# Sums in front of the remainders in the last groups of two square layers

## The chip, the cores and the metric

The kernel runs on one core of a Trainium2 chip. The metric is the device time of one execution in microseconds (us). A core has five engines that work side by side, each through its own queue: TensorE (PE, matrix products), VectorE (DVE), ScalarE (ACT), GpSimd (POOL) and SyncE (SP, which issues most of the DMAs here).

## What is computed

A transformer block on 4 batches of 1024 tokens with 256 features: attention with 16 heads, then a feed-forward part, each between a layer norm of its input and a layer norm of its output, with a residual. The change concerns the feed-forward part alone:

```python
def _tlin(x, w, s):
    return jnp.einsum('bsi,oi->bso', x, w) * s
h = jax.nn.silu(_tlin(x, w1_w, w1_s)) * _tlin(x, w2_w, w2_s)
h = jax.nn.gelu(_tlin(h, h1_w, h1_s), approximate=False)
h = jax.nn.gelu(_tlin(h, h2_w, h2_s), approximate=False)
return _tlin(h, w3_w, w3_s)
```

Features go 256 -> 1024 -> 1024 -> 1024 -> 256. `h1` and `h2` are the square layers. All weights `w*_w` are -1, 0 or 1.

## The kernel before

**Stages.** Attention takes the time to about 592 us. Then the feed-forward part runs batch after batch: `gated` (w1, w2, Silu and product), `Layer.run` for `h1`, `Layer.run` for `h2`, `finish` (w3, then the layer norm and the residual). In the first three batches the layer norm's last steps run within the next batch's `gated`; in the last batch (`b == B - 1`) `finish` runs them to the end, block by block, and stores.

**Precision.** [...] So each activation `raw` is split in two: `Operand.high` (line 923) rounds it on ScalarE (`hi`, line 925), `Operand.low` (line 927) takes the remainder `raw - hi` on VectorE (`lo`, line 929). Every product is done with both halves. A tile (`Half`) has 128 partitions x 1024 numbers: two blocks of 128 features by 512 tokens. Tiles come from a ring of free ones: `Half(...)` takes the oldest, `release` puts it back, in the order in which the program is written.

**A square layer** (`Layer`) treats input, weights and output as 2 x 2 blocks, (feature half i, token half j), and uses seven block products (`k` = 0 to 6) in place of eight. Which sums of weight blocks are used is prepared beforehand (`factors`, loaded from HBM into a ring of four slots by `load_factor`); the sums of input blocks are made on VectorE (`t1`, `make2`, `make3`, `make4`, line 941). Every product is done in two groups, `r` = 0 and 1, so a layer has 14 groups, `g` = 0 to 13. A group is 16 matmuls of 128x512 (line 1034) into a PSUM tile `ph`; there are three such tiles.

**Ends of groups.** After groups 6 and 7 a partial sum is kept (`keep_copy`, tile `w`); after groups 8 and 9 block (1,0) goes straight through Gelu (`straight`, tile `c`). After groups 10 to 13 stands `add` (line 1042): VectorE adds PSUM to a kept tile (line 1045), then ScalarE takes the Gelu in two halves (line 1022). Groups 10 and 11 give block (1,1) from `w`, groups 12 and 13 block (0,1) from `u`. Product 6 adds into the PSUM tile that product 5 began, so PE's group 12 (13) may start only when the sum of group 10 (11) has read that tile.

**Splits for the next layer.** While a layer's last groups run, its finished blocks are split for the next one. `ending` (line 1231) builds the lists: `early[g]` is run in group g after its matmuls are issued and before its sum, `extra[g]` after its sum and Gelu. Before the change, `early` holds both operations of a split, `high` then `low`. Half 1 of (0,0) is split in group 10, the halves of (1,0) in 11 and 12; in layer `h2` also half 0 of (1,1) in group 12 and half 1 in group 13, where half 0 of (0,1) follows in `extra`. The last one, half 1 of (0,1), is split in `finish` after the first scaling.

**The output** (`finish`). Four output tiles `pz` of 32 matmuls each (line 1139), token half 0 first. The products of token half 1 read block (1,1) first and (0,1) last. VectorE scales each (line 1144), and in the last batch goes on with the statistics, a root on POOL (line 107), the normalisation, the residual (line 1151) and a store.

Order on an engine is the order in which the program is written; each engine takes its queue from the front.

Of the kernel before, what the change touches and what calls it, by code (L numbers as in the profile page):

```python
# [129 lines left out]
def tile_fast(ctx: ExitStack, tc: tile.TileContext, x, wqk, wv, wo, w1, w1s, w2, w2s, h1, h1s, h2, h2s, w3, w3s, out, bad):  # L130
# [65 lines left out]
    with ExitStack() as actx, ExitStack() as rctx:  # L196
# [764 lines left out]
        def emit(runs):  # L961
            for run in runs:
                run()

        class Layer:
# [36 lines left out]
            def run(self, q, scale, extra, early):  # L1002

                out, at = self.out, {}
                hi, lo = self.high, self.low
                steps = {
                    0: [hi(2, 0), self.t1(1), self.make2(1), lo(2, 0)],
                    1: [hi(2, 1), lo(2, 1), self.make4(0), self.make4(1)],
                    2: [self.make3(0), self.make3(1), hi(3, 0), lo(3, 0)],
                    3: [hi(3, 1), lo(3, 1)],  # L1010
                    4: [hi(4, 0), lo(4, 0)],
                    5: [hi(4, 1), lo(4, 1)],
                    6: [hi(5, 0), lo(5, 0)],
                    7: [hi(5, 1), lo(5, 1)],
                    8: [hi(6, 0), lo(6, 0)],
                    9: [hi(6, 1), lo(6, 1)],
                }

                def gelu(o, i, r, src=None):
                    for j in range(2):  # L1020
                        m = HC // 2 * i + 2 * r + j
                        nc.scalar.activation(o.t[:, j, :], (o.t if src is None else src)[:, j, :], AF.Gelu, scale=scale[:, m : m + 1])  # L1022

                def space(r):
                    at[r] = ps.tile([P, 2, NQ], F32, tag="big", name="ph")
                    return at[r]

                def products(k, r, start):
                    p = at[r]
                    for c in range(HC // 2):  # L1030
                        for j in range(2):
                            w = ring_of[(q + k) % SLOTS][c // 2][:, c % 2, (2 * r + j) * P : (2 * r + j + 1) * P]
                            for n, half in enumerate(self.moving[k].pairs(c)):
                                nc.tensor.matmul(  # L1034
                                    p[:, j, :], w, half,
                                    start=start and c == n == 0, stop=c == HC // 2 - 1 and n == 1, skip_group_check=True,
                                )
                    if r:
                        self.moving[k].release()
                        load_factor(q + k + SLOTS)  # L1040

                def add(n, i, j, r):
                    o = out[n][r]
                    out.setdefault((i, j), []).append(o)
                    nc.vector.tensor_add(o.t, at[r], o.t)  # L1045
                    gelu(o, i, r)

                def keep_copy(n, r):
                    o = Half(n)
                    out.setdefault(n, []).append(o)  # L1050
                    nc.scalar.copy(o.t, at[r])

                def straight(i, r, p):
                    o = Half("c")
                    out.setdefault((i, 0), []).append(o)
                    gelu(o, i, r, p)

                def branch(r):
                    first[r] = at[r]
                    nc.scalar.copy(space(r), first[r])  # L1060

                first = {}

                def second(r):
                    p, at[r] = at[r], first[r]
                    products(1, r, False)
                    at[r] = p
                    straight(0, r, first[r])

                def after(g):  # L1070
                    emit(steps.get(g, ()))
                    emit(extra.get(g, ()))

                space(0), products(0, 0, True), branch(0), after(0)
                space(1), products(0, 1, True), after(1)
                second(0), branch(1), after(2)
                products(2, 0, False), keep_copy("u", 0), after(3)
                second(1), after(4)
                products(2, 1, False), keep_copy("u", 1), after(5)
                for g in range(6, 14):  # L1080
                    k, r = g // 2, g % 2
                    if k == 5:
                        space(r)
                    products(k, r, k == 5)
                    emit(early.get(g, ()))
                    if k == 3:
                        keep_copy("w", r)
                    elif k == 4:
                        straight(1, r, at[r])
                    else:  # L1090
                        add(*(("w", 1, 1) if k == 5 else ("u", 0, 1)), r)
                    after(g)
                return {n: out[n] for n in ((0, 0), (1, 0), (1, 1), (0, 1))}

# [127 lines left out]
        def feed_forward():  # L1222
# [8 lines left out]
            def ending(layer, drop):  # L1231
                for at in ((0, 0), (1, 0), (1, 1), (0, 1)):
                    layer.out[at] = []
                ops = {at: Operand(layer.out[at], drop) for at in ((0, 0), (1, 0), (1, 1), (0, 1))}
                extra = {g: [] for g in range(14)}
                extra[7] += split(ops[0, 0], 0)
                early = {g: split(ops[at], i) for g, at, i in ((10, (0, 0), 1), (11, (1, 0), 0), (12, (1, 0), 1))}
                return ops, extra, early

            def prepared(extra, steps):  # L1240
# [9 lines left out]
            for b in range(B):  # L1250
                last = b == B - 1
                x = {}
                for at in ((0, 0), (1, 0), (0, 1), (1, 1)):
                    x[at] = []
                corner, low = Operand(x[0, 0]), Operand(x[1, 0])
                one = Layer(x, corner, low)
                steps = {g: [] for g in range(NH * HC)}
                if b == 0:
                    for g in steps:
                        steps[g].append(side.take)  # L1260
                    steps[7].append(lambda: until(lambda: "fb" in ffn))
                for g, runs in tails.items():
                    steps[g] += runs
                for g, runs in (
                    (7 if b == 0 else 6, split(corner, 0)), (8 if b == 0 else 7, split(corner, 1)), (9, split(low, 0)), (11, split(low, 1)),
                    (12, [one.t1(0)]), (14, [one.make2(0)]),
                ):
                    steps[g] += runs
                if b == 1:
                    steps[6] += [checks.load, checks.load]  # L1270
                if b == 1:
                    checked(steps, (11,), (13,))
                elif b:
                    checked(steps, (1, 6, 11), (3, 8, 13))
                gated(x, steps)
                until(lambda: made_factors[0] == len(corners) and "fb" in ffn)
                q = 2 * 7 * b
                ops, extra, early = ending(one, False)
                if b == 0:
                    for g in range(3, 12):  # L1280
                        extra[g].append(side.take)
                if b:
                    checked(extra, (3, 4, 10), (5, 6, 12))
                if not last:
                    prepared(extra, prepare(2 * b + 2, to_scalar))
                if b == 0:
                    extra[5].insert(0, lambda: until(lambda: not chain[0]))
                y = one.run(q, scales["h1"], extra, early)
                until(lambda: not chain[0])
                two = Layer(y, ops[0, 0], ops[1, 0])  # L1290
                ops, extra, early = ending(two, True)
                if b:
                    checked(extra, (3, 4), (5, 6))
                if not last:
                    prepared(extra, prepare(2 * b + 3, to_scalar))
                else:
                    for g, step in zip((8, 9), judge()):
                        extra[g].append(step.run)
                early[12] += split(ops[1, 1], 0)
                early[13] = split(ops[1, 1], 1)  # L1300
                extra[13] += split(ops[0, 1], 0)
                emit([two.t1(0), two.make2(0)])
                two.run(q + 7, scales["h2"], extra, early)
                tails = finish(b, ops, {0: split(ops[0, 1], 1)})
# [333 lines left out]
```

## Time and profile before

| what | value |
|---|---|
| median of 3 runs (lowest, highest) | 1232.06 us (1228.26, 1233.94) |
| the profiled execution | 1232.08 us, its span 1230.2 us |
| granted clock of TensorE | 0.987 |
| PE busy in 595.0 to 757.4 us (batch 0) | 159.71 of 162.40 us |
| PE busy in 757.4 to 909.5 us (batch 1) | 151.17 of 152.10 us |
| PE busy in 909.5 to 1061.8 us (batch 2) | 151.34 of 152.30 us |
| PE busy in 1061.8 to 1211.0 us (batch 3) | 148.31 of 149.20 us |
| VectorE and ScalarE busy in batch 2 | 107.59 and 97.63 us |
| one remainder (line 929), one sum (line 1045) | 1.23 us, 1.22 us |
| a rounding (line 925), two Gelu halves (line 1022) | 1.04 us, 1.34 us |

The profile comes from one execution, so the times of its lines belong to the 1232.08 us. A row of the timeline gives the start, the duration, the engine, the line of the program, the operation, output and inputs by name, and in brackets the idle time of the engine before it with what ended that. When instructions of an engine follow closely, a row begins up to 0.1 us before the end of the row before it, so a queue is timed by the steps between starts. The 1.9 us between span and time of the execution lie around the span.

### The profile page before, as it was taken

To read this page: it belongs to the slowest core of one execution; us is meant where nothing else is said; L and a number is where in the kernel's file an instruction comes from. 1 tells how busy PE (TensorE), PEld (TensorE's weight loads), DVE (VectorE), ACT (ScalarE), POOL (GpSimd) and SP (SyncE) were. 2 spreads that over 40 slices of the span, in tenths; PEclk is the share of its full clock that TensorE was granted. 3 is DMA by queue.
4 is the path that set the end of the run, shared out by engine and by line. 5 is a ranking of instruction groups with operands and counts; after the bars stand their busy time and mean duration, and the time that the engine had idled before them with its cause. 6 is when DMAs were issued, how large, how long until landed. Compare 5 with 4: busy or idle time off the path is not lost.

```text
span 1230.2 us, 21266 instructions
## 1 busy us (share of the span) xinstructions
PE 1169.1 (95%) x7994; PEld 710.1 (58%) x7994; DVE 841.5 (68%) x1500; ACT 885.1 (72%) x1049; POOL 209.1 (17%) x279
## 2 busy tenths in 40 slices
PE   7999999999999999999999999999999999999993
PEld 2333333333333333333578888887888878888783
DVE  3485668777687756868685756867578676784755
ACT  3798899878988989999457565576656766566651
POOL 6222035434354432000000000000000000000000
PEclk8999999999999999999999999999999999999997
DMA  4676755756666666453314341344512545125401
GB/s 132 175 183 152 172 148 134 186 135 175 152 162 154 173 168 148 96 140 128 104 34 138 119 156 52 103 171 147 178 59 97 175 156 176 62 82 199 155 7 37
DMA packets 78672, 163.66 MB, mean 133 GB/s; under 512 B 14688, under 2 KB 40928, under 8 KB 78560
## 3 DMA queue, kind: packets, MB, share of 16 engines
q1 hardware_dynamic: 68624, 131.27, 38.7%
q0 software_dynamic: 9408, 30.42, 7.7%
q8 instruction: 65, 1.06, 0.4%
q10 hardware_dynamic: 528, 0.52, 0.2%
q14 instruction: 47, 0.39, 0.1%
HBM read 98.71 MB, written 29.88 MB: 105 GB/s over the span
## 4 chain that ended last, share of the span: by engine, by line
PE 58%; DVE 12%; ACT 12%; SPq 6%; DMA 6%; issue 5%; ACTq 0%; POOL 0%; POOLq 0%; DVEq 0%
PE ph L1034 27%; PE acc L542 9%; PE pg L955 8%; ACT e L535 6%; PE s L534 6%; SPq L482 5%; PE p L321 3%; DVE lo L929 2%; ACT hi L925 2%; PE py L321 2%; DVE top L554 1%; DMA sq<-cq1lo 1%; DMA folded<-top_d 1%; PE pz L1139 1%; DVE w L1045 1%
## 5 line engine op out<-in xcount | busy, mean ns | idle before, releaser
L535 ACT ACTIVATE e<-s 128x1024 f32<-128x1024 f32 x512 | 483.1, 1043 | 53.8 <-PE s L534 44.1
L542 PE MATMUL acc<-e,vaug 128*32 128x512 f32 (+1 forms) x2424 | 258.7, 539 | 2.9 <-POOL vaug L512 2.9
L534 PE MATMUL s<-sq,sk 64*128 64x512 f32 x1024 | 189.3, 446 | 25.3 <-ACT e L535 17.1
L534 PEld LDWEIGHTS s<-sq,sk 64*128 64x128 f32 x1024 | 87.6, 185 | 172.0 <-ACT e L535 142.1
L1034 PE MATMUL ph<-hi,sq 128*128 128x512 f32 x448 | 178.1, 398 | 0.8 <-DVE w L1045 0.8
L1034 PE MATMUL ph<-lo,sq 128*128 128x512 f32 x448 | 176.7, 394 | 0.0
L1034 PE MATMUL ph<-hi,sk 128*128 128x512 f32 x448 | 176.7, 394 | 0.0
L1034 PE MATMUL ph<-lo,sk 128*128 128x512 f32 x448 | 176.4, 394 | 0.0
L107 POOL TENSOR_TENSOR rstd<-ve,minus_half 128x4 f32<-128x4 f32 (+1 forms) x34 | 38.2, 1123 | 740.6 <-DVE ve L105 681.8
L554 DVE TENSOR_TENSOR top<-top,e 128x512 f32<-128x512 f32 x192 | 138.9, 723 | 24.3 <-ACT e L535 18.5
L542 PEld LDWEIGHTS acc<-e,vaug 128*32 128x32 f32 x2424 | 61.8, 109 | 120.5 <-issue 107.8
L929 DVE TENSOR_TENSOR lo<-c,hi 128x1024 fp32r<-128x1024 f32 x48 | 58.4, 1223 | 66.0 <-ACT hi L925 66.0
L929 DVE TENSOR_TENSOR lo<-g,hi 128x1024 fp32r<-128x1024 f32 x48 | 58.8, 1226 | 58.0 <-ACT hi L925 57.7
L1034 PEld LDWEIGHTS ph<-hi,sq 128*128 128x128 f32 x448 | 84.2, 188 | 21.6 <-DVE w L1045 2.1
L1034 PEld LDWEIGHTS ph<-hi,sk 128*128 128x128 f32 x448 | 84.1, 188 | 20.0
L1034 PEld LDWEIGHTS ph<-lo,sk 128*128 128x128 f32 x448 | 84.1, 188 | 19.9
L1034 PEld LDWEIGHTS ph<-lo,sq 128*128 128x128 f32 x448 | 84.2, 188 | 19.1
L1022 ACT ACTIVATE c<-ph,h_scale 128x512 f32<-128x512 f32 x64 | 40.6, 685 | 50.1 <-PE ph L1034 50.1
L321 PE MATMUL p<-xT,wqk_sb 128*32 128x512 f32 x512 | 69.3, 622 | 4.7 <-ACT wqk_sb L209 2.6
L957 ACT ACTIVATE sg<-pg,w_scale 128x512 f32<-128x512 f32 x64 | 43.6, 688 | 35.7 <-PE pg L955 31.9
L1139 PE MATMUL pz<-w_sb,lo 128*128 128x256 f32 x256 | 61.6, 284 | 2.8 <-DVE lo L929 2.8
L958 DVE SCALAR_TENSOR_TENSOR g<-pg,w_scale,sg 128x512 f32<-128x512 f32 x64 | 47.7, 747 | 23.1 <-ACT sg L957 23.0
(183 smaller groups left out, 1735.1 us busy)
## 6 DMA issues: line engine op xcount, KB each, us to landing
sq<-h_f SPq DMA_DIRECT2D x56, 512.0 KB, 3.8
sk<-h_f SPq DMA_DIRECT2D x56, 512.0 KB, 4.5
w<-in_h_dram POOLq DMA_DIRECT2D x32, 256.0 KB, 5.2
h_f<-wr POOLq DMA_DIRECT2D x16, 512.0 KB, 4.3
x<-in_h_dram SPq DMA_DIRECT2D x16, 512.0 KB, 3.6
top_d<-top SPq DMA_DIRECT2D x30, 256.0 KB, 2.5
folded<-top_d SPq DMA_DIRECT2D x30, 256.0 KB, 3.2
h_f<-wr POOLq DMA_DIRECT2D x16, 384.0 KB, 3.7
```

What stands on the lines that cost most here:

```text
L321: nc.tensor.matmul(o[j : j + SLOT, :], w[:, j : j + SLOT], i, **flags)
L482: queue.dma_start(out=stacks[w, i, u][o : o + DH, c0:c1].bitcast(F32), in_=cq[w, m, k][r : r + DH, c0:c1].bitcast(F32))
L534: nc.tensor.matmul(s[:, a, :], stacks[1, g % 2, u][r, c * P : (c + 1) * P], stacks[0, g % 2, u][r, h * NQ : (h + 1) * NQ], start=True, sto ...
L535: nc.scalar.activation(pair(k)[:, u], s, AF.Exp)
L542: nc.tensor.matmul(acc[SLOT * i : SLOT * (i + 1), q0:q1], vaug[g % 2][:, c, i, :], pair(k)[:, i // 2, i % 2, q0:q1], start=c == 0 and q0 = ...
L554: nc.vector.tensor_max(top, top if c > 1 else pair(k - 2)[:, :, :, 0:P], pair(k)[:, :, :, 0:P])
L929: nc.vector.tensor_sub(self.lo[i].t, self.raw[i].t, self.hi[i].t.bitcast(F32))
L955: nc.tensor.matmul(p[:, k, :], homes[n][d][:, m * P : (m + 1) * P], half[:, d, :], start=d == j == 0, stop=d == DC - 1 and j == 1)
L957: nc.scalar.activation(sg, p[:, 0, :], AF.Silu, scale=scales["w1"][:, m : m + 1])
L958: nc.vector.scalar_tensor_tensor(x[i, h][c // 2].t[:, c % 2, :], p[:, 1, :], scales["w2"][:, m : m + 1], sg, ALU.mult, ALU.mult)
L1034: nc.tensor.matmul(p[:, j, :], w, half, start=start and c == n == 0, stop=c == HC // 2 - 1 and n == 1, skip_group_check=True,)
L1139: nc.tensor.matmul(p[:, j, :D], half[:, (t0 + j) * P : (t0 + j + 1) * P], homes["w3"][c], start=c == order[0] and n == 0, stop=c == order[ ...
```

## The change

In groups 6 to 13 the roundings of `early[g]` stay in front of the group's own sum or Gelu, and the remainders move behind it. `early` holds pairs of an operand and a half in place of functions. In layer `h2`, half 0 of block (0,1), which was split after the sum of group 13, joins the list of that group, so that its rounding stands before that group's Gelu. The number of instructions stays the same on every engine. For this shape, ScalarE's order differs in one rounding per batch, VectorE's in the remainders of groups 10 to 13 against the sums; the orders on PE, POOL and SP are the same.

```diff
@@ -1082,13 +1082,16 @@
                     if k == 5:
                         space(r)
                     products(k, r, k == 5)
-                    emit(early.get(g, ()))
+                    for o, i in early.get(g, ()):
+                        o.high(i)
                     if k == 3:
                         keep_copy("w", r)
                     elif k == 4:
                         straight(1, r, at[r])
                     else:
                         add(*(("w", 1, 1) if k == 5 else ("u", 0, 1)), r)
+                    for o, i in early.get(g, ()):
+                        o.low(i)
                     after(g)
                 return {n: out[n] for n in ((0, 0), (1, 0), (1, 1), (0, 1))}
 
@@ -1234,7 +1237,7 @@
                 extra[7] += split(ops[0, 0], 0)
-                early = {g: split(ops[at], i) for g, at, i in ((10, (0, 0), 1), (11, (1, 0), 0), (12, (1, 0), 1))}
+                early = {g: [(ops[at], i)] for g, at, i in ((10, (0, 0), 1), (11, (1, 0), 0), (12, (1, 0), 1))}
                 return ops, extra, early
 
@@ -1296,9 +1299,8 @@
-                early[12] += split(ops[1, 1], 0)
-                early[13] = split(ops[1, 1], 1)
-                extra[13] += split(ops[0, 1], 0)
+                early[12].append((ops[1, 1], 0))
+                early[13] = [(ops[1, 1], 1), (ops[0, 1], 0)]
                 emit([two.t1(0), two.make2(0)])
                 two.run(q + 7, scales["h2"], extra, early)
                 tails = finish(b, ops, {0: split(ops[0, 1], 1)})
```

## The prediction

> **What bounds the kernel now.** I began with the page: per engine, TensorE (PE) is busy for 95% of the span, VectorE (DVE) for 68%, ScalarE (ACT) for 72%. The slices of the feed-forward part (from about 592 us on) show PE at nine tenths or more and its clock at nine, except in the last slice. So two places can pay: the few gaps in PE, and the end, where PE is done and others finish.
>
> ```profile
> PE 1169.1 (95%) x7994; PEld 710.1 (58%) x7994; DVE 841.5 (68%) x1500; ACT 885.1 (72%) x1049; POOL 209.1 (17%) x279
> PE   7999999999999999999999999999999999999993
> L929 DVE TENSOR_TENSOR lo<-c,hi 128x1024 fp32r<-128x1024 f32 x48 | 58.4, 1223 | 66.0 <-ACT hi L925 66.0
> ```
>
> The third line says that a remainder (`lo`) takes 1223 ns and that VectorE sat idle for 66 us in front of 48 of them, waiting for a rounding (`hi`) on ScalarE. Idle time of VectorE costs nothing by itself, so I went on to the timeline of the last layer's groups 10 to 13 (batch 3, `h2`), VectorE and then ScalarE:
>
> ```profile
> 1185.24 1.21 DVE L1045 TENSOR_TENSOR w<-ph,w 128x1024 f32<-128x1024 f32 x1
> 1188.79 1.23 DVE L929 TENSOR_TENSOR lo<-c,hi 128x1024 fp32r<-128x1024 f32 x1 [2.35 <-ACT hi L925]
> 1189.93 1.22 DVE L1045 TENSOR_TENSOR w<-ph,w 128x1024 f32<-128x1024 f32 x1
> 1193.49 1.23 DVE L929 TENSOR_TENSOR lo<-c,hi 128x1024 fp32r<-128x1024 f32 x1 [2.34 <-ACT hi L925]
> 1194.63 1.22 DVE L929 TENSOR_TENSOR lo<-w,hi 128x1024 fp32r<-128x1024 f32 x1
> 1195.77 1.22 DVE L1045 TENSOR_TENSOR u<-ph,u 128x1024 f32<-128x1024 f32 x1
> 1200.47 1.22 DVE L1045 TENSOR_TENSOR u<-ph,u 128x1024 f32<-128x1024 f32 x1
> 1205.18 0.68 DVE L1144 TENSOR_TENSOR z<-pz,w3s_sb 128x512 f32<-128x512 f32 x1
> ...
> 1186.48 1.34 ACT L1022 ACTIVATE w<-w,h_scale 128x512 f32<-128x512 f32 x2 [2.67 <-DVE w L1045]
> 1187.72 1.04 ACT L925 CAST hi<-c 128x1024 fp32r<-128x1024 f32 x1
> 1191.18 1.34 ACT L1022 ACTIVATE w<-w,h_scale 128x512 f32<-128x512 f32 x2 [2.43 <-DVE w L1045]
> ```
>
> Read it as a loop over two engines. The sum (L1045) at 1185.24 releases the Gelu (1186.48); the rounding stands behind that Gelu on ScalarE; the remainder waits for the rounding (1188.79); the next sum stands behind the remainder on VectorE (1189.93). One turn is 1.24 + 2.31 + 1.14 = 4.69 us, and the turn of group 12, with two remainders, 5.84 us. PE's groups take 16 matmuls of 0.232 us, 3.71 us (its first matmul of group 11 is at 1184.51, of group 12 at 1188.22). So the sums fall behind PE: PE ends group 10 at 1184.67 and its sum starts 0.57 us later; PE ends group 13 at 1195.84 and its sum starts at 1200.47, 4.63 us later. The first output product (`pz`) is complete near 1199.7, and its scaling (L1144) comes at 1205.18.
>
> Third, the waits from 590 us on, and one of PE's gaps in its timeline:
>
> ```profile
> PE pz L1139 <- DVE lo L929: 2.8, 7, 0.5
> PE ph L1034 <- DVE w L1045: 0.8, 3, 0.4
> ...
> 1054.78 0.28 PE L1139 MATMUL pz<-w_sb,hi 128*128 128x256 f32 x1
> 1055.23 0.38 PE L1139 MATMUL pz<-w_sb,lo 128*128 128x256 f32 x1 [0.18 <-DVE lo L929]
> 1055.45 0.28 PE L1139 MATMUL pz<-w_sb,hi 128*128 128x256 f32 x1
> ```
>
> These two rows are PE's idle time due to this loop. Idle time is counted from an overlapping, modelled end, so I price a gap by the step between starts: here 0.45 us where 0.117 is usual, and 0.22 for the step after it.
>
> **What the Trainium skill says.** "PSUM — Partial Sum Buffer", Engine vs sequencer instructions: the queues of ScalarE and VectorE are strict FIFO. The trace agrees: the sum at 1189.93 starts as the remainder ends, though PE had finished group 11 at 1188.39. "VectorE: DVE Perf Modes", The TRN2 errata: an fp32 `tensor_tensor` takes (N+151)/0.96 ns, an estimate of 1224 ns for N = 1024; the trace has 1223. "Perfetto Trace Analysis", Optimization Strategy: find the gaps on the engine that should be saturated and what they wait for; that is the third view.
>
> **The change, part by part.**
>
> 1. *Order on VectorE.* No instruction is added or removed. Built, the two programs differ on ScalarE and VectorE alone: PE, POOL and SP have the same instructions in the same order, so no DMA moves. In groups 10 to 13 a sum now stands in front of the remainders of its group. The loop is open: sum g waits for PE and for the sum before it, no longer for the Gelu of g-1. Per group VectorE has a sum and a remainder, 1.22 + 1.14 = 2.36 us, in group 12 3.50 us; ScalarE has a Gelu pair and a rounding, 1.24 + 0.95 = 2.19, in groups 12 and 13 one rounding more, 3.14. All are under PE's 3.71, so sums should keep up with PE.
>
> 2. *Walked through the last layer* with PE's times of before and the durations above: sums at 1184.7, 1188.4, 1192.1 and 1195.9 (the last formerly 1200.47); Gelus 1.25 us behind each; remainders of group 12 at 1193.3 and 1194.5, ending 1195.6, 0.2 us before the last sum; then two remainders, ending 1198.2 and 1199.4; the scaling at 1199.7, as soon as PE has the product; the last remainder ends at 1201.5 (formerly 1207.0).
>
> 3. *The rounding that is moved.* The diff moves one rounding as well: `hi` of block (0,1), half 0, goes from behind the last Gelu to in front of it. On ScalarE it runs from 1195.7 to 1196.7; the Gelu cannot start before its sum ends at 1197.1. Cost 0; without that cover it would be 0.95 us in each of four layers, 3.8 us at most. Its buffer comes from the ring of free halves; following the ring in both programs, no half in these groups comes from a later reader on PE than the group just finished.
>
> 4. *Gaps in PE.* In the layers `h1` of batches 1 to 3, PE's group 13 must wait until the group-11 sum has read the same PSUM tile: steps of 0.62, 0.65 and 0.75 us against 0.23, and the next step 0.33 each. Together 1.33 + 0.31 = 1.64 us. At the output products of batches 0 to 2, two gaps each for `lo` of block (0,1): steps 0.69, 0.78, 0.46, 0.79, 0.45, 0.81 against 0.117, together 3.28, and the six steps after them 0.66 more, 3.94 us. By part 2 both sums and remainders come 3 to 5 us earlier, more than any gap. PE has no other work to wait for there; bound 0 below, 5.58 above, and I take 5.58, since the walk leaves spare time everywhere. Batch 3's gap is in the end below.
>
> 5. *The end.* From the scaling at 1205.18 to the last of four blocks VectorE runs a chain with a wait for POOL in every block (5.58 us for the first, which contains a remainder, 4.57 for the others), and the span ends 5.6 us after its last addition. All of it hangs on the first scaling, which comes 1205.18 - 1199.7 = 5.48 us earlier. What is late next: PE ends its fourth product at 1195.68 + 128 x 0.117 = 1210.7, and its scaling would come at 1219.91 - 5.48 = 1214.4, so 3.7 us to spare. Bound 0 below, 5.48 above; I take 5.48.
>
> 6. *Queued behind the waiting sums.* The remainder behind a sum that waits for PE comes up to 1.2 us later than it could. Its earliest reader is the first output product at three quarters: the remainder of (1,0) ends at 1194.5, PE reads it at 1195.68 + 24 x 0.117 = 1198.5. In `h1` the remainders' first reader is group 0 of the next layer, over three groups (11 us) on. Cost 0.
>
> Sum: 5.58 + 5.48 = 11.1 us from 1232.08 (the profiled execution, span 1230.2 and 1.9 around it), which is 0.02 above the median of the runs: **1221.0 us**.
>
> **Rivals.** *One of the two parts only.* If PE's gaps stay, because the last remainder is late for another reason, 1232.08 - 5.48 = 1226.6; if the end stays, because the scaling waits for something else than VectorE's queue, 1232.08 - 5.58 = 1226.5. For it: gaps and end are separate waits. Against: one lag of 4.63 us explains both.
> *The queue blocks at its head (slower).* VectorE stands at a sum waiting for PE with finished roundings behind it; where PE reads a remainder at once, it waits for a sum and a remainder, 2.36 us, at eight ends of layers: 1232.08 + 18.9 = 1251. It decides once a remainder lags more than the 4.0 us of part 6. Against: 2.36 of 3.71 us are used per group; for: 3.50 of 3.71 in group 12.
> *It does nothing that can be seen*, if the order is not what binds: 1232. The repeated turns of 4.69 us speak against it.
>
> **How the numbers follow.** Both parts 0.83 (1221.0); one part 0.11 (1226.5, which is 0.45% below, of which a third falls over the 0.5% line by scatter); nothing 0.02; slower 0.04. No change is within 0.5%, 6.2 us, about what a measurement of this kernel can tell. So faster 0.87, same 0.09, slower 0.04. Range: the likeliest gain has an upper bound, so the low end is scatter alone (runs before lay 3.8 below to 1.9 above the median), 1217.5; the high end takes in one part alone, 1227.
>
> **What would show it.** In the timeline the last sum within 0.2 us of PE's last `ph`; the first scaling 5 us earlier against it; no wait of PE `pz` for `lo` nor of `ph` for `w`; idle time before L929 for the Gelu's rounding smaller. I am wrong if PE shows new waits for `lo` at layer starts, or the scaling moves less than 4 us.

## The result and the profile after

The median went from 1229.82 us (1226.38 to 1233.94, 7 runs) to 1218.03 us (1216.37 to 1222.22, 7 runs). The ratio is 0.9908, 95% interval 0.989 to 0.9926: 11.3 us less by the ratio (9.1 to 13.5 by the interval), where 11.1 were forecast. The profiled execution took 1217.59 us, its span 1215.7.

The profile's summary, and from it the remainders' group (`fp32r` in a row is the rounded type of `hi` and `lo`):

```profile
PE 1162.8 (96%) x7994; PEld 708.4 (58%) x7994; DVE 841.0 (69%) x1500; ACT 885.8 (73%) x1049; POOL 207.8 (17%) x279
PE   7899999999999999999999999999999999999995
L929 DVE TENSOR_TENSOR lo<-c,hi 128x1024 fp32r<-128x1024 f32 x48 | 58.2, 1219 | 25.8 <-ACT hi L925 25.8
```

Every engine runs the same number of instructions as before. What changed is in the last column of the third line: VectorE's wait for a rounding in front of these 48 remainders fell from 66.0 to 25.8 us.

The timeline of the last layer's groups 10 to 13, VectorE, then ScalarE (below line 1093 the changed file is three lines longer, so the scaling is L1147):

```profile
1175.83 1.23 DVE L1045 TENSOR_TENSOR w<-ph,w 128x1024 f32<-128x1024 f32 x1 [0.49 <-PE ph L1034]
1179.54 1.22 DVE L1045 TENSOR_TENSOR w<-ph,w 128x1024 f32<-128x1024 f32 x1 [1.35 <-PE ph L1034]
1180.68 1.22 DVE L929 TENSOR_TENSOR lo<-c,hi 128x1024 fp32r<-128x1024 f32 x1
1183.27 1.23 DVE L1045 TENSOR_TENSOR u<-ph,u 128x1024 f32<-128x1024 f32 x1 [1.38 <-PE ph L1034]
1184.41 1.22 DVE L929 TENSOR_TENSOR lo<-c,hi 128x1024 fp32r<-128x1024 f32 x1
1185.55 1.22 DVE L929 TENSOR_TENSOR lo<-w,hi 128x1024 fp32r<-128x1024 f32 x1
1186.98 1.23 DVE L1045 TENSOR_TENSOR u<-ph,u 128x1024 f32<-128x1024 f32 x1 [0.21 <-PE ph L1034]
1190.71 0.69 DVE L1147 TENSOR_TENSOR z<-pz,w3s_sb 128x512 f32<-128x512 f32 x1 [0.24 <-PE pz L1142]
...
1186.71 1.04 ACT L925 CAST hi<-u 128x1024 fp32r<-128x1024 f32 x1
1188.24 1.34 ACT L1022 ACTIVATE u<-u,h_scale 128x512 f32<-128x512 f32 x2 [0.48 <-DVE u L1045]
```

Look at the brackets. Before, remainders waited for ScalarE and sums for nothing the view showed, since they stood behind the remainders. Now each of these sums waits for PE alone (`PE ph`), the sums are 3.71 to 3.73 us apart like PE's groups, and the remainders shown have no wait. After two remainders in group 12 the wait is 0.21 us: the work of that group just fits. The scaling waits for PE's product.

The waits of the feed-forward part say the same. Two rows are new, in which VectorE's 32 sums wait for PE, 16 and 15 times (the second number is how often, the first the total in us):

```profile
DVE w L1045 <- PE ph L1034: 13.6, 16, 1.4
DVE u L1045 <- PE ph L1034: 13.4, 15, 1.4
```

and the two rows of before in which PE waits, for `lo` at the output products and for `w` in a layer, are gone.

To place the gain, I cut each profile by the starts of three instructions in its timeline: the first gated matmul (`pg`), the first output matmul (`pz`) of batch 3, the first scaling of batch 3.

| stretch, us | before | after | difference |
|---|---|---|---|
| start to first `pg` (attention) | 594.78 | 591.74 | -3.04 |
| A: first `pg` to batch 3's first `pz` | 600.90 | 595.04 | -5.86 |
| B: that `pz` to the first scaling | 9.50 | 3.94 | -5.56 |
| C: the first scaling to the end of VectorE's last instruction | 24.99 | 24.99 | 0.00 |

The two profiled executions differ by 14.49 us, but 3.04 of them lie in attention, whose instructions the change does not touch. In the ten profiles of this study that stretch ends anywhere from 587.68 to 596.97 us, while A and B repeat to 0.2 us where the code is the same. C contains the stores and repeats to 0.3 us. The end of the last addition, measured from the first scaling, repeats to 0.03 us (19.36 to 19.39) in seven of the eight profiles in which the last steps of the program are unaltered; the eighth, with 19.78, is the third experiment, and is read there. So small effects are read below from A, B and C, and whole times serve as a check.

### The profile page after: what moved, and what is told of

It is laid out like the page before. It is cut to its first block, busy times and chain, and to the rows that moved or that the text cites. A ratio compares the mean times of both kernels' runs of the same rounds, so it can differ in the third digit from the quotient of the medians.

```text
span 1215.7 us, 21265 instructions
## 1 busy us (share of the span) xinstructions
PE 1162.8 (96%) x7994; PEld 708.4 (58%) x7994; DVE 841.0 (69%) x1500; ACT 885.8 (73%) x1049; POOL 207.8 (17%) x279
## 4 chain that ended last, share of the span: by engine, by line
PE 69%; ACT 10%; DVE 9%; DMA 4%; SPq 3%; issue 3%; ACTq 0%; POOL 0%; POOLq 0%; DVEq 0%
PE ph L1034 34%; PE acc L542 10%; PE pg L955 8%; ACT e L535 8%; PE s L534 6%; PE pz L1142 4%; PE p L321 3%; SPq L482 2%; DVE top L554 2%; PE py L321 2%; DMA x<-in_x_dram 1%; PE pv L321 1%; DMA sq<-cq1lo 1%; DVE st L97 1%; PE fpt L898 1%
## 5 line engine op out<-in xcount | busy, mean ns | idle before, releaser
L929 DVE TENSOR_TENSOR lo<-c,hi 128x1024 fp32r<-128x1024 f32 x48 | 58.2, 1219 | 25.8 <-ACT hi L925 25.8
L1142 PE MATMUL pz<-w_sb,hi 128*128 128x256 f32 x256 | 60.0, 279 | 0.0
```

Of the source, the lines that this page charges most:

```text
L929: nc.vector.tensor_sub(self.lo[i].t, self.raw[i].t, self.hi[i].t.bitcast(F32))
L1142: nc.tensor.matmul(p[:, j, :D], half[:, (t0 + j) * P : (t0 + j + 1) * P], homes["w3"][c], start=c == order[0] and n == 0, stop=c == order[ ...
```

## The experiments

**One layer at a time.** The new order in `h1` alone, and in `h2` alone (`q % 14` is 0 in `h1` and 7 in `h2`; shown is `h1` alone):

```diff
+                    late = q % 14 == 0
                     for o, i in early.get(g, ()):
                         o.high(i)
+                        if not late:
+                            o.low(i)
...
-                    for o, i in early.get(g, ()):
-                        o.low(i)
+                    if late:
                         for o, i in early.get(g, ()):
                             o.low(i)
```

With `h1` alone, half 0 of (0,1) is also split after the last Gelu again.

> Only the layers h1 have the new order; h2 is as in the kernel before. Three stretches of a profile: A, from the first gated matmul (first pg) to the first output matmul of batch 3 (pz), 600.9 us before and 595.0 us after the change; B, from there to the first scaling, 9.50 before and 3.94 after; C, from the scaling to the end of the span, 24.98 in both. My theory (two separate waits, PE's ph behind the sums of h1, and PE's pz and the last scaling behind the remainders of h2): PE's waits of ph for the sum are gone, A 599.2 (1.7 us less than before), B 9.5, about 1.7 us faster than before. Rival (one part brings it all, h1's order also lets h2 begin earlier): A near 595, or B clearly below 9.5.

Measured: A 599.22, B 9.50; median 1227.88 us, ratio 0.998 (0.9966 to 0.9993) to the kernel before. PE's waits from the first gated matmul on:

```profile
PE pz L1146 <- DVE lo L929: 2.8, 7, 0.5
PE pg L955 <- DVE g L958: 1.8, 2, 1.0
```

The waits of `pz` are all there, seven of them as before; those of `ph` are gone. (The second row is in the kernel before too.)

> Only the layers h2 have the new order; h1 is as in the kernel before. My theory: PE's waits of ph for the sum stay (3 gaps), those of pz for the remainder go; A 596.7 (4.2 us less than before), B 3.9, C 25.0; about 9.7 us faster than before and 1.7 slower than the changed kernel. Rival (the sums are not what holds h1): A as in the changed kernel, 595.0.

Measured: A 596.68, B 3.94; median 1219.26 us, ratio 0.9911 (0.9892 to 0.993). PE's waits:

```profile
PE pg L955 <- DVE g L958: 1.8, 2, 1.0
PE ph L1034 <- DVE w L1045: 0.9, 3, 0.3
```

Now the three waits of `ph` are there and those of `pz` gone. The two layers' shares add up: 1.68 of A from `h1`, 4.22 of A and all of B from `h2`, 5.90 against the 5.86 of both. Neither rival held.

**The last group alone**, `late = q % 14 == 7 and g == 13`. This asks whether the end needs the loop of groups 10 to 13 to be opened, or only the last sum to pass the last remainder.

> Only group 13 of the layers h2 has the new order (its sum in front of its remainder, the rounding of (0,1) half 0 in front of its Gelu); groups 10 to 12 are as before. My theory, a loop that lags a little more in every group: sum 12 still comes 4 us late, sum 13 follows it at once, B about 5.9 (3.6 of the 5.6 us), the gaps of pz gone in batches 0 to 2 (A 596.7), about 7.8 us faster than before. Rival 1 (only the last sum's place counts): B 3.9, as with all groups changed. Rival 2 (the order has to be changed in every group, or the loop stays closed): B 9.5, A 600.9.

Measured: A 596.82, B 5.97; median 1222.27 us, ratio 0.9937 (0.9922 to 0.9953). VectorE's timeline:

```profile
1182.31 1.22 DVE L1045 TENSOR_TENSOR w<-ph,w 128x1024 f32<-128x1024 f32 x1
1185.88 1.23 DVE L929 TENSOR_TENSOR lo<-c,hi 128x1024 fp32r<-128x1024 f32 x1 [2.34 <-ACT hi L925]
1187.02 1.22 DVE L929 TENSOR_TENSOR lo<-w,hi 128x1024 fp32r<-128x1024 f32 x1
1188.15 2.35 DVE L1045 TENSOR_TENSOR u<-ph,u 128x1024 f32<-128x1024 f32 x2
```

The sum of group 12 comes 5.84 us after that of group 11 (1188.15 against 1182.31), as before, and the sum of group 13 directly behind it (the last row merges both). So group 13 alone takes 3.53 of the 5.56 us in B and the gaps of `pz`; the other 2.03 us were lag from the groups before it. Both rivals miss by about 2 us or more; the lag builds up over the groups.

What is left of the lag reaches ScalarE too, and beyond the scaling. The last remainder waits for its rounding there:

```profile
1194.99 1.23 DVE L929 TENSOR_TENSOR lo<-u,hi 128x1024 fp32r<-128x1024 f32 x1 [0.31 <-ACT hi L925]
```

The last addition therefore ends 19.78 us after the first scaling in place of 19.37. Up to that addition, group 13 alone brings 3.14 of 5.58 us.

**The moved rounding.** The change moves one rounding on ScalarE besides the remainders. Moved back:

```diff
-                early[13] = [(ops[1, 1], 1), (ops[0, 1], 0)]
+                early[13] = [(ops[1, 1], 1)]
+                extra[13] += split(ops[0, 1], 0)
```

> The changed kernel with the rounding of (0,1) half 0 behind the last Gelu again, as before. My prediction put the move at no cost and did not count a gain for it. Walked through with the durations of the changed kernel, the remainder that needs this rounding would end at 1191.7 in place of 1190.5 on that profile's clock and hold the first scaling, which PE has ready at 1190.7: B 4.8 to 4.9 in place of 3.94, A 595.0, so 0.9 us slower than the changed kernel. Rival (the move is worth nothing, the scaling is bound by PE alone): B 3.94.

Measured: A 595.19, B 4.91; median 1218.73 us, ratio 0.9923 (0.9897 to 0.9948). By whole times it can't be told from the changed kernel; by B it is 0.97 us slower. Its timeline on VectorE:

```profile
1185.85 1.22 DVE L929 TENSOR_TENSOR lo<-w,hi 128x1024 fp32r<-128x1024 f32 x1
1188.27 1.23 DVE L929 TENSOR_TENSOR lo<-u,hi 128x1024 fp32r<-128x1024 f32 x1 [1.21 <-ACT hi L925]
1189.41 0.68 DVE L1147 TENSOR_TENSOR z<-pz,w3s_sb 128x512 f32<-128x512 f32 x1
```

The remainder of (0,1) waits 1.21 us for its rounding, which now stands behind the Gelu, and holds the scaling behind it. So of B's 5.56 us, 0.97 hang on the rounding, once the order on VectorE is the new one. The moved rounding alone, with the old order on VectorE, was not run.

**More work in the tight group.** Group 12 has 3.50 us of VectorE work against 3.71 on PE. To find where the slower rival would begin, its second remainder is taken again, once and four times more (the same values each time):

```diff
+                    if q % 14 == 7 and g == 12:
+                        for _ in range(1):    # and 4
+                            nc.vector.tensor_sub(o.lo[i].t, o.raw[i].t, o.hi[i].t.bitcast(F32))
```

> The changed kernel with one more VectorE instruction per batch: in group 12 of h2 the second remainder is taken twice (same result), so that this group asks VectorE for 4.64 us in place of 3.50, against 3.71 on PE. My theory (the queue is free of the loop, and only work over PE's time per group shows): the last sum 0.9 us later against PE's last ph, B 4.5 in place of 3.94, A 595.0. Rival (VectorE is hidden under PE): B 3.94. Rival (a sum waiting at the queue's head costs PE time): new waits of PE, A over 597.

Measured: A 594.91, B 4.57; one execution, 1217.71 us.

> The same with four more, 8.06 us of VectorE in group 12. My theory: the last sum 4.3 us late, B 7.9, and still no wait of PE for a remainder, since the last one would end 0.6 us before PE reads it: A 595.0, so 4.0 us slower than the changed kernel, in the end alone. Rival (VectorE is hidden under PE): B 3.94. Rival (slower, the head of the queue blocks): PE waits at pz in every batch, A over 597.

Measured: A 595.09, B 8.34; one execution, 1217.9 us (attention ended early in it, at 587.68).

```profile
1182.79 5.00 DVE L1097 TENSOR_TENSOR lo<-w,hi 128x1024 fp32r<-128x1024 f32 x4
1187.71 1.22 DVE L1045 TENSOR_TENSOR u<-ph,u 128x1024 f32<-128x1024 f32 x1
```

The last sum (1187.71) comes directly behind the repeats, with no wait for PE. The end moves by 0.63 and 4.40 us, a little more than the 0.56 and 4.0 expected, because a repeat starts 1.25 to 1.26 us after the remainder before it, not 1.14. PE has no wait for `lo` in either, so over four batches A stays. The changed kernel's sums wait 27.0 us in all at the head of the queue, and PE waits for no remainder there either. So in this kernel a waiting sum cost nothing by itself; work beyond PE's time per group did, and only at the very end. One repeat (1.26 us of the queue) moves B by 0.63, four (5.03 us) by 4.40: 0.6 us of added work fits before the scaling is late.

**What is late next.** If the end is VectorE's chain, it should shrink when the chain does. First, in batch 3, the last remainder goes behind the first block's statistics, into the wait for the root on POOL:

```diff
-                    emit(after.get(2 * h + t0 // 2, ()))
                     if b == B - 1:

                         ln = norms.stats([z[:, t, :] for t in range(t0, t0 + 2)])
+                        emit(after.get(2 * h + t0 // 2, ()))
...
+                    emit(after.get(2 * h + t0 // 2, ()))
```

> The changed kernel, and in batch 3 the last remainder stands behind the first block's statistics, where VectorE waits 0.9 us for the root on POOL. Theory that the end is VectorE's chain: C 24.1 in place of 24.98, A and B as in the changed kernel. Rival (the end is bound by the stores or by PE's last product): C 24.98.

Measured: A 594.99, B 3.94, C 24.36, and the second scaling 5.39 us after the first in place of 5.58; median 1215.71 us, ratio 0.9884 (0.9865 to 0.9902). The last addition comes 19.16 us after the first scaling in place of 19.37: on VectorE only 0.2 us of 0.9 were won. (The rest of C's fall lies behind the last addition, in a stretch of 5.20 us that takes 5.34 to 5.72 us in the eight profiles with unaltered last steps.) Why so little is read from the root on POOL. VectorE's remainder and POOL's root here:

```profile
1197.40 1.22 DVE L929 TENSOR_TENSOR lo<-u,hi 128x1024 fp32r<-128x1024 f32 x1
1197.65 1.51 POOL L107 TENSOR_TENSOR rstd<-ve,minus_half 128x2 f32<-128x2 f32 x1 [136.06 <-DVE ve L105]
1199.21 0.41 DVE L126 TENSOR_SCALAR z<-z,mv,rstd 128x256 f32<-128x256 f32 x1 [0.59 <-POOL rstd L107]
```

and the same root in the changed kernel:

```profile
1193.99 0.70 POOL L107 TENSOR_TENSOR rstd<-ve,minus_half 128x2 f32<-128x2 f32 x1 [137.07 <-DVE ve L105]
```

The root took 1.51 us beside the remainder, 0.70 alone. The wait that was to be filled grew.

Second, each block's normalisation and residual also go behind the next block's scaling and statistics (`complete` holds the lines taken out, and `held` is run once more after the last block):

```diff
                     if b == B - 1:

                         ln = norms.stats([z[:, t, :] for t in range(t0, t0 + 2)])
-                        for j, t in enumerate(range(t0, t0 + 2)):
...
+                        emit(after.get(2 * h + t0 // 2, ()))
+                        emit(held)
+                        held = [lambda h=h, t0=t0, z=z, ln=ln: complete(h, t0, z, ln)]
                         continue
```

> The same, and in batch 3 each block's normalisation and residual stand behind the next block's scaling and statistics, so that VectorE does not wait for POOL. The changed kernel has 5.58 + 3 x 4.57 us from the first scaling to the fourth, PE delivers a product every 3.75 us. Theory that VectorE's chain sets the end: with PE's product at its back the fourth scaling 11.3 us after the first, the last addition 2.8 us earlier, C 22.2; about 2.8 us faster than the changed kernel and 14 faster than the kernel before. Rival (the stores or PE bound the end): C stays near 25.

Measured: A 595.00, B 3.94, C 21.94; median 1216.25 us, ratio 0.9896 (0.9877 to 0.9915) to the kernel before.

```profile
1195.91 0.69 DVE L1158 TENSOR_TENSOR z<-pz,w3s_sb 128x512 f32<-128x512 f32 x1 [0.24 <-PE pz L1153]
1199.65 0.69 DVE L1158 TENSOR_TENSOR z<-pz,w3s_sb 128x512 f32<-128x512 f32 x1 [0.51 <-PE pz L1153]
1203.41 0.69 DVE L1158 TENSOR_TENSOR z<-pz,w3s_sb 128x512 f32<-128x512 f32 x1
1207.17 0.69 DVE L1158 TENSOR_TENSOR z<-pz,w3s_sb 128x512 f32<-128x512 f32 x1
```

The scalings are 3.74 to 3.76 us apart, PE's time for a product, where they were 4.57 to 5.58. PE sets the pace now: the first two rows wait for it, and the last two start 0.04 us after PE's third and fourth products end (1203.37 and 1207.13). The last addition comes after 16.48 us, 2.89 earlier (2.8 expected), and C is 3.05 us shorter than in the changed kernel. Its A, B and C sum to 620.88 us against 623.97. The whole times of the two, 1216.25 and 1218.03, lie too close, for the scatter of attention, to show this by themselves.

## Why the prediction was right

*The loop over two engines* (views and part 1): shown. With the order changed, sums follow PE's groups of 3.71 us, and the third experiment catches the loop half closed, with the lag of 5.84 us per turn in group 12 still in it.

*The walk through the last layer* (part 2): sums, remainders and scaling came where it put them, counted from PE. Last sum: forecast right at the end of PE's group 13, measured with a wait of 0.21 us for PE. Scaling: forecast 4.0 us behind the first `pz` (1199.7 against 1195.68), measured 3.94. Last remainder: ends 5.8 us behind it in the forecast, 5.76 measured.

*The moved rounding* (part 3): mis-sized. I priced what it might cost, 0, and gave it no credit; it earns 0.97 us of B. The forecast of B was still right, because the walk had the rounding in its new place. What part 3 missed is that without the move only 4.59 of the 5.56 us come.

*PE's gaps* (part 4): 1.64 us were forecast for `ph`, and `h1` alone brought 1.68; 3.94 for `pz`, and `h2` alone brought 4.22 of A. The 0.28 us between 3.94 and 4.22 are the largest miss in the sum: the gaps were added up from single steps, and the stretches of output products in batches 0 to 2 became shorter by 1.64, 1.39 and 1.22 us, 4.25 in all. Where within them the rest lies was not followed up.

*The end* (part 5): 5.48 forecast, 5.56 measured, all of it in B. C did not change, as forecast. That C hung on VectorE, and not on PE or the stores, was argued then and is shown by the last experiment.

*The waits at the queue's head* (part 6 and the slower rival): no cost for PE, and none appears in A even with 8 us of work in group 12. The rival of one part only is refuted by the first two experiments: both parts came, from two places.

The time lies 3.0 us below the forecast of 1221.0. Of this, 2.2 is the kernel before, whose median over seven runs is 1229.82 and not the 1232.06 of the three runs on which the forecast stood; so the time lies only 0.5 us above the low end of the range, 1217.5. The remaining 0.7 is the gain, 11.8 by the two medians against 11.1. A and B put the gain at 11.42, so about half of the 0.7 is scatter of whole runs.

## What to carry to other kernels

Where two in-order engines hand work to each other twice within a group, see what stands in front of what on each queue: an operation that waits for the other engine, put in front of one that needs only TensorE, ties group g to group g-1, and the lag adds up over the groups while no engine is full. Put first what frees the bottleneck or starts the other engine's next piece, and last what is read late; then check that the work per group fits the bottleneck's time per group, since beyond that limit (here 0.2 us before the last sum is late, 0.6 before the scaling is) every instruction shows at the end. And where one stage's scatter is larger than the effect, compare the stretches between marked instructions rather than whole times.

## What the runs showed of the hardware

The root on POOL, two numbers per partition, took 1.51 us in both of the last two experiments, where a VectorE remainder with two inputs in SBUF (the on-chip memory that holds the tiles) started about 0.25 us before it, and 0.70 us otherwise; it ended about 0.55 us after the remainder's row. I had counted that wait as free to fill. Such a pair was there to see in the kernel before: in batch 0 a root over four numbers starts 0.05 us after a remainder and takes 2.05 us, where the other roots of the first three batches take 1.01.

```profile
626.05 1.23 DVE L929 TENSOR_TENSOR lo<-g,hi 128x1024 fp32r<-128x1024 f32 x1
626.10 2.05 POOL L107 TENSOR_TENSOR rstd<-ve,minus_half 128x4 f32<-128x4 f32 x1 [13.33 <-DVE ve L105]
```

The Trainium skill, "SBUF — State Buffer", SBUF: two separate sides, says that a VectorE operation with two SBUF inputs and a GpSimd operation that reads SBUF exclude each other for a whole instruction, whichever starts first. The profiles fit that where the root starts second. Where it starts first they do not: six remainders of the kernel before started 0.80 to 0.91 us into a root of 1.01 us and took their usual 1.23 us. In the last experiment three additions of the residual, with two SBUF inputs too, started 0.18 us into a root; they took 0.42 to 0.43 us as elsewhere, and the roots 0.70. So in these runs only a root that started behind such an operation was lengthened. Times on POOL are rough in a profile, but VectorE's own wait agrees with the 1.51 us: in the first of the two experiments it went on 0.05 us after the root's end (1199.21 against 1199.16).
